# Layer 0's gate and up products by a scheme of seven products for eight, with Silu in both halves

## The chip, the cores and the metric

The kernel runs on one core of one Trainium2 chip. The metric is the device time of one execution in microseconds (us): the median of several runs, beside one execution taken with the hardware profiler. The engines are TensorE (PE; its weight loads are listed as PEld), VectorE (DVE), ScalarE (ACT), GpSimd (POOL) and SyncE (SP, which issues most DMAs). Each runs its own instructions in order; they wait for each other by semaphores.

## What is computed

Two layers on x of shape (4, 256, 256), all in float32. Layer 0 is an attention of 16 heads and a gated feed-forward; layer 1 is an mLSTM with a gated feed-forward of its own, and then a feed-forward with int8 weights. The change is in layer 0's feed-forward (`fwht` is a normalized Walsh-Hadamard transform; W1 and W3 are 1024 x 256):

```python
up_gate = jnp.einsum('bsd,hd->bsh', x, W1)
up_lin = jnp.einsum('bsd,hd->bsh', x, W3)
hidden = jax.nn.silu(up_gate) * up_lin
hidden = fwht(hidden)
out = jnp.einsum('bsh,dh->bsd', hidden, W2)
...
x = _layernorm(x + _L0_attn_ref(x, ...), axis=-1)
x = _layernorm(x + _L0_ffn_ref(x, ...), axis=-1)
x = _layernorm(x + _L1_attn_ref(x, ...), axis=-1)
x = _layernorm(x + _L1_ffn_ref(x, ...), axis=-1)
```

## The kernel before

The 1024 tokens are two halves of 512 tokens, that is of two batches of 256. P is 128, KC = 2 chunks of the 256 features, NH = 8 chunks of the 1024 hidden features.

**Attention, 0 to about 407 us.** It goes by 16 blocks, one for each pair of heads and half. The projections of the next block (`fast_projections`) already use a scheme of seven products for eight: a 2x2 block product, over two output chunks and two batches, is built from seven block products with sums of inputs (`input_sums`, kept in `xsum`) and of weights (`weight_sums`, kept in `wsums`, on VectorE at the end of every even block). Each partial result accumulates in one of two PSUM banks, "x" and "y"; ScalarE copies what is in x to where it is wanted, VectorE adds what is in y. The steps A1 to A7 and B1 to B7 are issued in an order written out by hand (`ORDER`, and `EARLY` for blocks 0 and 1), between the scores, the products with the values (V) and the output products (O). Block 1 uses `EARLY[1]`. The banks of the B steps (tag "sc") are those that block 1's first scores lie in. GpSimd does the rotary products (L298 to L300) and, before the last block, the Hadamard butterflies of W2 between chunks; four matrix products (`hadamard`) do those within a chunk, the last two at about 408 us.

**Layer 0's feed-forward** (`ffn0`, with `glu` and `down`) is written as a generator for each half: layernorm, transposes, then for every hidden chunk two products of 512 columns for the gate and two for the up part, a Tanh on ScalarE, (tanh + 1) times the gate and times the up part on VectorE (silu(v) is v/2 times (tanh(v/2) + 1); the half is taken in `down`), then four rows of eight down products of 256 columns. Half 0's up part (410 to 437 us) runs by itself.

**Half 1 and the mLSTM.** Half 1's stream is filler for the first half of the mLSTM. `merge` takes the number that `mlstm` yields, which is how many microseconds of other TensorE work should stand there, and pulls pieces from the other stream until their own yields (1.7 for half a chunk of `glu` or half a row of `down`) have paid it; the program order comes out of these counts. The engines' queues follow it, except where something later was ready first. `mlstm(0)` asks for 9.0, 1.7, 0, 1.7, 1.7, 3.4, 1.7, 3.4, 9.0 and 1.7, and 4.3 more are asked for after it, around the norm with which `ffn1(0)` begins. What then is left of the stream follows the transposes of `ffn1(0)`. After that, `ffn1(0)` is filler for `mlstm(1)` in the same way.

**ScalarE in the mLSTM.** `gates` needs Exp, Ln and Exp after a Tanh; `decays` needs 8 Exps of 128x128 in each of four groups. A group is queued behind the newest gate activation traced so far (`evictions[-1]`, L1003). GpSimd prepares the Exps' input (L995), from maxima that come back by DMA.

**Buffers.** Weights and sums of 8 KB a partition share the tag "ff" with seven buffers, each taken when one is free, in program order. ScalarE's functions are read from a table; when the one that is wanted isn't in the table that is loaded, an ACT_TABLE_LOAD stands before it.

Of the kernel before, what the change touches and what calls it, by code (L numbers as in the profile page):

```python
# [25 lines left out]
NH = FF // P  # L26
HALF = NT // 2
NJH = HALF // P
# [11 lines left out]
def tile_two_layers(ctx: ExitStack, tc: tile.TileContext, a: dict, out: bass.AP):  # L40
    nc = tc.nc
# [5 lines left out]
    def bank(tag):  # L47
        return psum.tile([P, 512], F32, tag=tag, name=f"ps_{tag}")
# [90 lines left out]
    def ff_weight(name, engine=nc.sync, dtype=F32):  # L139

        tiled = [P, NH, D] if name in ("w2", "w_down", "q_down") else [P, KC, FF]
        t = wts.tile(tiled, dtype, tag="ff", name=name, bufs=7)
        src = a[name]
        engine.dma_start(t, src.bitcast(mybir.dt.int8) if src.dtype == I32 else src)
        return t

    xsum = wts.tile([P, 2, 4, S], F32, tag="ff", name="xsum", bufs=7)
    wsums = [wts.tile([P, 4, 4 * P], F32, tag="ff", name=f"wsum{k}", bufs=7) for k in range(2)]
# [10 lines left out]
    settled = {}  # L159
    behind = lambda ins: tc.issue_after(ins.ins)  # L160
    nothing = lambda: None

    def projections(h):

# [367 lines left out]
    def output_product(h, bb, po):  # L532
# [24 lines left out]
    ORDER = "A1 A2 V00 A6 V01 A7 A5 B1 B2 A3 A4 B6 B7 V10 B5 V11 O0 B3 O0 B4 O1 O1".split()  # L557
    EARLY = {
        0: "A1 A2 B1 A6 B2 A7 A5 B6 A3 B7 B5 A4 B3 B4".split(),
        1: "A1 A2 B1 B2 A6 A7 B6 B7 A5 B5 V00 A3 V01 A4 B3 B4 V10 V11 O0 O0 O1 O1".split(),  # L560
    }
    def fast_block(h, t, probs, prev, steps):

# [66 lines left out]
    for h in range(NB - 1):  # L630
        if h and h % 2 == 0 and h // 2 + 1 < NPAIR:
            with behind(settled["block"]):
                weight_sums(h // 2 + 1)
        probs = fast_block(h, tiles, probs, prev, steps)
        if h % 2 == 0:
            if 0 < h < NB - 2:
                w_os[h // 2 + 1] = load_output(h // 2 + 1)
            if h // 2 + 2 < NPAIR:
                weights[h // 2 + 2] = load_pair(h // 2 + 2)
        prev, tiles = tiles, after_it  # L640
        if h + 2 < NB:
            after_it, steps = fast_projections(h + 2)

# [153 lines left out]
            nc.vector.tensor_tensor(hT[:, c, :], pu, g, ALU.mult)  # L797
            yield 1.7

    def down(hT, wd, j, tag, rows):  # L800

        po = bank(tag)[:, :D]
        for i in range(NH):
            nc.tensor.matmul(  # L804
                po, lhsT=hT[:, i, j * P : (j + 1) * P], rhs=wd[:, i, :], start=(i == 0), stop=(i == NH - 1)
            )
            if i == NH // 2 - 1:
                yield 1.7
        with tc.issue_after(chained[-1].ins) if chained else contextlib.nullcontext():
            nc.vector.scalar_tensor_tensor(rows, po, 0.5, rows, ALU.mult, ALU.add)  # L810
        yield 1.7

    def ffn0(n, tag):
        fm, hT = feature_major(n), hidden(n, hid)
        layernorm(acc[n], acc[n])
        yield 0.0
        transposed(acc[n], fm, tag)
        yield 0.9
        yield from glu(fm, w1, w3, hT, tag)
        for j in range(NJH):  # L820
            yield from down(hT, w2h, j, tag, acc[n][:, j, :])
        layernorm(acc[n], xb[n])

    def ffn1(n, tag):

        h2 = work.tile([P, NJH, D], F32, tag="hin", name=f"h2_{n}")
        rmsnorm(acc[n], h2)
        yield 0.0
        fm, hT = feature_major(n), hidden(n, hid)
        evicted = transposed(h2, fm, tag, vecs[:, 4:6])  # L830
        with tc.issue_after(evicted.ins):
            for j in range(NJH):
                nc.vector.tensor_tensor(xs[n][:, j, :], acc[n][:, j, :], xb[n][:, j, :], ALU.add)
        yield 0.9
        yield from glu(fm, w_gate, w_up, hT, tag)
        for j in range(NJH):
            yield from down(hT, w_down, j, tag, xs[n][:, j, :])
            if j % 2:
                layernorm(xs[n][:, j - 1 : j + 1], xb[n][:, j - 1 : j + 1], 2)

# [15 lines left out]

    def mlstm_in(n, t):

        hin = work.tile([P, NJH, D], F32, tag="hin", name=f"hin{n}")
        rmsnorm(xb[n], hin)  # L860
        yield 10.5 if n else 9.0
        fm = feature_major(n)
# [209 lines left out]
    def run(stream):  # L1072
        for _ in stream:
            pass

    def take(count, stream):
        return itertools.islice(stream, count)
# [160 lines left out]
            yield from s  # L1238

    hid = tc.alloc_tile_pool(name="hid", bufs=2)  # L1240
    up = 2 + 2 * NH
# [137 lines left out]
```

## Time and profile before

| what | value |
|---|---|
| median of 3 runs | 697.17 us (694.35 to 697.26) |
| the profiled execution | 697.11 us, span 695.3 us |
| mean granted TensorE clock | 0.992 |
| ScalarE busy, 409.8 to 437.2 us (half 0's gate and up) | 5.5 us |
| ScalarE busy, 451.9 to 526.2 us (half 1 with the mLSTM) | 28.2 us |
| VectorE busy, 451.9 to 526.2 us | 51.2 us |
| table loads of ScalarE | 7 in all: one at the start, four in the mLSTM, two in the last feed-forward |
| HBM read | 25.61 MB, 38 GB/s over the span |

The profile's page gives the busy time of each engine as a share of the span, the chain of work that ended last, and groups of instructions by line, engine and operation. A line of a timeline has start (us), duration (us), engine, source line, operation, output and inputs with their shapes, and how many records were merged; an idle time before it stands in brackets with what ended it. A wait line has who waited for whom: us in total, times, the longest. The products of the helper that all of them share are at L70, so they are told apart by their tiles: `ps_d` is a PSUM bank of the feed-forwards, `ps_m` of the mLSTM.

### The profile page before, as it was taken

The numbers are of one execution on the slowest core, as the hardware profiler recorded it, in microseconds if no ns is written. First come the engines' busy times: TensorE is split into PE (matmuls) and PEld (weight loads), VectorE is DVE, ScalarE is ACT, GpSimd is POOL, SyncE is SP. The second block draws the span as 40 slices with busy tenths as digits, with TensorE's granted clock in tenths as the row PEclk, the third lists the DMA queues.
The fourth block names the chain that finished last, engine by engine and source line by source line (L and its number), as shares of the span: only waits on it lengthen the run. The fifth ranks groups of instructions, "written<-read, shape, count | busy, mean of one in ns | idle before, by whom it ended". The sixth has DMA issues, their size and how long they took to land.

```text
span 695.3 us, 9871 instructions
## 1 busy us (share of the span) xinstructions
PE 685.8 (99%) x3408; PEld 533.6 (77%) x3408; DVE 451.3 (65%) x1242; ACT 260.3 (37%) x773; POOL 177.4 (26%) x187
## 2 busy tenths in 40 slices
PE   9999999999999999999999999999999999999995
PEld 5888988988888898888889764845685458648885
DVE  5966666577478568567547664273779459835767
ACT  2442543354254244325425331037212561111652
POOL 4244404422730740742143000005000130000210
PEclk9999999999999999999999999999999999999998
DMA  8543233332321521531432451003030300000001
GB/s 271 213 122 60 42 96 61 59 94 46 84 85 30 136 47 22 131 61 24 113 62 39 144 106 27 0 1 122 1 122 0 123 1 1 0 0 1 1 0 61
DMA packets 49026, 45.43 MB, mean 65 GB/s; under 512 B 9520, under 2 KB 42704, under 8 KB 47824
## 3 DMA queue, kind: packets, MB, share of 16 engines
q1 hardware_dynamic: 48112, 41.00, 22.8%
q0 software_dynamic: 432, 3.15, 1.3%
q10 hardware_dynamic: 432, 0.66, 0.3%
q8 instruction: 27, 0.44, 0.3%
q14 instruction: 23, 0.19, 0.1%
HBM read 25.61 MB, written 1.08 MB: 38 GB/s over the span
## 4 chain that ended last, share of the span: by engine, by line
PE 97%; DVE 2%; ACT 1%; issue 0%; DVEq 0%; ACTq 0%
PE ps_mm L354 13%; PE ps_d L70 12%; PE ps_mm L70 9%; PE ps_m L70 8%; PE ps_ot L70 8%; PE ps_sc L346 6%; PE ps_sc L354 6%; PE ps_d L804 6%; PE ps_sc L438 4%; PE ps_pt L438 4%; PE ps_d L1117 4%; PE ps_sc L450 2%; PE ps_m L1036 2%; PE ps_m L804 2%; PE ps_pt L450 2%; PE ps_m L773 1%
## 5 line engine op out<-in xcount | busy, mean ns | idle before, releaser
L298 POOL TENSOR_TENSOR rope_raw<-rope_raw,cst 128x512 f32<-128x512 f32 x30 | 38.2, 1274 | 187.8 <-DVE rope_swp L295 187.8
L470 ACT ACTIVATE pr<-ps_sc,nmax 128x256 f32<-128x256 f32 x64 | 29.7, 474 | 121.3 <-DVE nmax L461 121.3
L70 PE MATMUL ps_mm<-w_o,oT 128*128 128x256 f32 x256 | 62.2, 379 | 0.0
L70 PE MATMUL ps_ot<-prT,v 128*128 128x256 f32 x240 | 61.4, 380 | 0.2 <-issue 0.2
L70 PE MATMUL ps_d<-fm,w 128*128 128x512 f32 x128 | 58.1, 606 | 0.0
L552 DVE TENSOR_TENSOR acc<-ps_mm,acc 128x512 f32<-128x512 f32 x32 | 22.1, 691 | 49.8 <-PE ps_mm L70 49.6
L70 PEld LDWEIGHTS ps_mm<-w_o,oT 128*128 128x128 f32 x256 | 46.7, 190 | 5.3
L995 POOL TENSOR_TENSOR ex<-cst,ex 128x512 f32<-128x512 f32 x16 | 19.7, 1263 | 110.8 <-DMA ex<-far 66.1
L70 PEld LDWEIGHTS ps_ot<-prT,v 128*128 128x128 f32 x240 | 43.3, 190 | 5.5 <-issue 0.9
L70 PEld LDWEIGHTS ps_d<-fm,w 128*128 128x128 f32 x128 | 24.2, 192 | 27.5 <-issue 25.6
L461 DVE TENSOR_REDUCE nmax<-ps_sc 128x2 f32<-128x512 f32 x32 | 20.6, 685 | 36.2 <-PE ps_sc L450 36.0
L354 PE MATMUL ps_mm<-xsum,wsum 128*128 128x256 f32 x180 | 43.9, 380 | 0.0
L488 DVE STREAM_TRANSPOSE cross<-pr 128x512 f32<-128x512 f32 x60 | 42.6, 710 | 1.4
L368 ACT COPY kn<-ps_sc 128x256 f32<-128x256 f32 x56 | 20.9, 373 | 58.3 <-PE ps_sc L346 58.2
L480 DVE TENSOR_SCALAR pr<-pr,rinv 128x256 f32<-128x256 f32 x128 | 39.1, 347 | 1.6
L795 ACT ACTIVATE glu_g<-ps_d 128x512 f32<-128x512 f32 x24 | 14.2, 594 | 67.8 <-PE ps_d L70 67.8
L299 POOL TENSOR_TENSOR rope_swp<-rope_swp,cst 128x512 f32<-128x512 f32 x30 | 38.2, 1275 | 0.0
L354 PEld LDWEIGHTS ps_mm<-xsum,wsum 128*128 128x128 f32 x180 | 33.9, 190 | 4.5
L377 DVE TENSOR_TENSOR kn<-ps_sc,kn 128x256 f32<-128x256 f32 x42 | 17.8, 424 | 28.6 <-ACT kn L368 18.1
L1113 POOL TENSOR_TENSOR qh<-gq,qh 128x512 fp32r<-128x512 f32 x6 | 7.8, 1294 | 96.4 <-issue 84.7
L470 ACT ACTIVATE pr<-ps_pt,nmax 128x256 f32<-128x256 f32 x64 | 30.1, 488 | 2.5 <-DVE nmax L461 2.5
L438 PE MATMUL ps_sc<-kn,qn 128*128 128x256 f32 x128 | 30.2, 379 | 0.0
(271 smaller groups left out, 1567.0 us busy)
## 6 DMA issues: line engine op xcount, KB each, us to landing
prT<-cross SPq DMA_DIRECT2D x240, 64.0 KB, 2.1
w_qkv<-in_w_qkv SPq DMA_DIRECT2D x7, 1024.0 KB, 5.4
ex<-far SPq DMA_DIRECT2D x8, 512.0 KB, 5.6
w<-in_w SPq DMA_DIRECT2D x3, 1024.0 KB, 12.4
w_o<-in_w_o SPq DMA_DIRECT2D x8, 256.0 KB, 3.0
acc<-in_x SPq DMA_DIRECT2D x2, 512.0 KB
w_gate<-in_w_gate SPq DMA_DIRECT2D x1, 1024.0 KB
w_up<-in_w_up SPq DMA_DIRECT2D x1, 1024.0 KB, 5.1
```

Source lines behind the costliest of these rows:

```text
L70: last = nc.tensor.matmul(ps, lhsT=lhs(i), rhs=rhs(i), start=(i == 0), stop=(i == n - 1))
L298: nc.gpsimd.tensor_tensor(by_b(raw[c]), by_b(raw[c]), cs, ALU.mult)
L299: nc.gpsimd.tensor_tensor(by_b(swp), by_b(swp), sn, ALU.mult)
L346: lambda: nc.tensor.matmul(ps[:, k * S + j * P : k * S + (j + 1) * P], lhsT=x[:, j * P : (j + 1) * P], rhs=wt, start=(start and not k and ...
L354: lambda: nc.tensor.matmul(ps[:, k * S : (k + 1) * S], lhsT=wt, rhs=x, start=(start and not k), stop=True, skip_group_check=True,)
L438: lambda: nc.tensor.matmul(ps[bb][e][:, qt * S : (qt + 1) * S], lhsT=qn[:, e, queries(bb, qt)], rhs=kn[:, e, keys(bb)], start=(qt == 0), s ...
L450: lambda: nc.tensor.matmul(ps[bb][e][:, qt * S : (qt + 1) * S], lhsT=qr[rows, queries(bb, qt)], rhs=kr[rows, keys(bb)], start=False, stop= ...
L470: nc.scalar.activation(pr[:, qt, :], ps[:, qt * S : (qt + 1) * S], AF.Exp, bias=nmax[:, qt : qt + 1], accum_out=rsum[:, qt : qt + 1],)
L480: nc.vector.tensor_scalar(pr[:, qt, :], pr[:, qt, :], rinv[:, qt : qt + 1], None, ALU.mult)
L488: return nc.vector.transpose(cross[:, :, e], pr.rearrange("p t (x i) -> p x t i", i=32))
L804: nc.tensor.matmul(po, lhsT=hT[:, i, j * P : (j + 1) * P], rhs=wd[:, i, :], start=(i == 0), stop=(i == NH - 1))
L1117: nc.tensor.matmul(ps, lhsT=lhs, rhs=rhs, start=(k == 0), stop=(k == len(terms) - 1))
```

## The change

Layer 0's gate and up products take the scheme of seven products that the attention has. A "pair" is two hidden chunks; for each of the four pairs, each of the seven products is made for the gate and for the up weights, over 256 columns. Gate and up share a bank. `fast_glu` steps through the pairs in an order written out by hand (`STEPS`: first digit the pair, second the product); "--" pulls the first half of the first down row forward.

```diff
+    def hidden_sums(engine, ws, which):
+        for x, w in enumerate(ws):
+            part = lambda i, c: w[:, i, :].rearrange("p (k c d) -> p k c d", c=2, d=P)[:, :, c, :]
+            one, two = gsum[:, 0, x], gsum[:, 1, x]
+            if which == "first":
+                engine.tensor_tensor(one, part(0, 1), part(1, 1), ALU.add)
+                engine.tensor_tensor(two, one, part(0, 0), ALU.subtract)
+            elif which == "third":
+                engine.tensor_tensor(gsum3[:, x], part(0, 0), part(0, 1), ALU.subtract)
+            else:
+                engine.tensor_tensor(part(0, 1), part(1, 0), two, ALU.subtract)
...
-        1: "A1 A2 B1 B2 A6 A7 B6 B7 A5 B5 V00 A3 V01 A4 B3 B4 V10 V11 O0 O0 O1 O1".split(),
+        1: "A1 A2 A6 A7 B1 B2 A5 B6 B7 B5 V00 A3 V01 A4 B3 B4 V10 V11 O0 O0 O1 O1".split(),
...
+        if h == NB - 3:
+            gsum = wts.tile([P, 2, 2, NH // 2, P], F32, tag="ff", name="gsum", bufs=7)
+            with behind(settled["block"]):
+                hidden_sums(nc.vector, (w1, w3), "first")
...
+    gsum3, tsum = more_sums()
+    for which in ("third", "fourth"):
+        hidden_sums(nc.gpsimd, (w1, w3), which)
...
-    w_gate, w_up = ff_weight("w_gate"), ff_weight("w_up")
-    w_down = ff_weight("w_down")
+    w_up, w_gate = ff_weight("w_up"), ff_weight("w_gate")
...
+    def token_sums(xT):
+        tok = lambda i, b: xT[:, i, b * S : (b + 1) * S]
+        one, two, three, four = (tsum[:, m, :] for m in range(4))
+        nc.vector.tensor_tensor(one, tok(0, 1), tok(0, 0), ALU.subtract)
+        nc.vector.tensor_tensor(two, tok(1, 1), one, ALU.subtract)
+        nc.vector.tensor_tensor(three, tok(1, 1), tok(0, 1), ALU.subtract)
+        return nc.vector.tensor_tensor(four, tok(1, 0), two, ALU.subtract)
+
+    STEPS = (
+        "01 02 11 06 12 07 05 16 17 03 04 15 21 22 13 26 14 27 25 31 32 23 36 37 24 35 -- 33 34"
+    ).split()
+
+    def fast_glu(xT, wg, wu, hT, tag, silu, other):
+        def pair(k):
+            g, banks, batch = [], {}, lambda b: slice(b * S, (b + 1) * S)
+            def products(name, m):
+                start = m in (1, 2, 7)
+                if m < 3:
+                    banks[name] = bank(tag)
...
+                    nc.tensor.matmul(
+                        banks[name][:, batch(x)], lhsT=left, rhs=right,
+                        start=start and not x, stop=True, skip_group_check=True,
+                    )
...
+            def copy(c, b):
+                for x, to in enumerate(places(c, b)):
+                    nc.scalar.copy(to, banks["x"][:, batch(x)])
+            def add(c, b):
+                for x, to in enumerate(places(c, b)):
+                    nc.vector.tensor_tensor(to, banks["y"][:, batch(x)], to, ALU.add)
+            def gated(c, b, found=None):
+                gate, to = places(c, b)
+                at_g, at_u = found or (gate, to)
+                if silu:
+                    evictions.append(nc.scalar.activation(gate, at_g, AF.Silu))
+                else:
+                    th = gate if found else work.tile([P, S], F32, tag="junk", name="glu_th")
+                    evictions.append(nc.scalar.activation(th, at_g, AF.Tanh, scale=0.5))
+                    nc.vector.scalar_tensor_tensor(gate, th, 1.0, at_g, ALU.add, ALU.mult)
+                nc.vector.tensor_tensor(to, at_u, gate, ALU.mult)
+            def step(m):
+                products("x" if m in (1, 6, 5, 3) else "y", m)
+                if m == 1:
+                    copy(0, 0)
+                elif m == 2:
+                    add(0, 0)
+                    gated(0, 0)
+                elif m == 6:
+                    copy(1, 0)
+                elif m == 5:
+                    copy(1, 1)
+                    add(1, 1)
+                    gated(1, 1)
+                elif m == 3:
+                    gated(0, 1, (banks["x"][:, batch(0)], banks["x"][:, batch(1)]))
+                elif m == 4:
+                    add(1, 0)
+                    gated(1, 0)
+            return step
+        pairs = [pair(k) for k in range(NH // 2)]
+        for s in STEPS:
+            if s == "--":
+                yield next(other)
+            else:
+                pairs[int(s[0])](int(s[1]))
+                yield 0.86
...
-        yield from glu(fm, w1, w3, hT, tag)
+        token_sums(fm)
+        silu = True
+        rows = [down(hT, w2h, j, tag, acc[n][:, j, :], 1.0 if silu else 0.5) for j in range(NJH)]
+        yield from fast_glu(fm, w1, w3, hT, tag, silu, rows[0])
...
-        h2 = work.tile([P, NJH, D], F32, tag="hin", name=f"h2_{n}")
+        h2 = work.tile([P, NJH, D], F32, tag="hin", name=f"h2_{n}", bufs=1)
...
-    run(take(up - 2, one))
+    run(take(len(STEPS), one))
...
-    q_gate, q_up, q_down = (ff_weight(k, nc.gpsimd, F32R) for k in ("q_gate", "q_up", "q_down"))
+    w_down = ff_weight("w_down")
+    q_gate, q_up = (ff_weight(k, nc.gpsimd, F32R) for k in ("q_gate", "q_up"))
...
+    q_down = ff_weight("q_down", nc.gpsimd, F32R)
     run(take(1 + 2 * NH + 2 * NJH - 3, one))
```

The fourth weight sum overwrites the weight block that it replaces. `gsum`, and one buffer for `gsum3` and the token sums `tsum`, take two of the seven "ff" buffers. So layer 1's weights come into other buffers, and some later. The layer 1 feed-forward keeps `glu` with its Tanh.

More of the change, by code (lines that the diff above doesn't have):

```diff
@@ L145, in ff_weight @@
         return t
+    pair_sums = lambda k: wts.tile([P, 4, 4 * P], F32, tag="ff", name=f"wsum{k}", bufs=7)
+    wsums = [pair_sums(0)]
     xsum = wts.tile([P, 2, 4, S], F32, tag="ff", name="xsum", bufs=7)
-    wsums = [wts.tile([P, 4, 4 * P], F32, tag="ff", name=f"wsum{k}", bufs=7) for k in range(2)]
+    wsums.append(pair_sums(1))
     w2b = wts.tile([P, NH, D], F32, tag="ff", name="w2b", bufs=7)
@@ L161, in tile_two_layers, with more_sums @@
     nothing = lambda: None
+    def more_sums():
+        both = wts.tile([P, 8 * S], F32, tag="ff", name="gsum3", bufs=7)
+        return (
+            both[:, 0 : 4 * S].rearrange("p (x k d) -> p x k d", x=2, k=NH // 2),
+            both[:, 4 * S :].rearrange("p (m s) -> p m s", m=4),
+        )
[10 more added lines that the diff above has]
+                engine.tensor_tensor(part(0, 1), part(1, 0), two, ALU.subtract)
     def projections(h):
@@ L798, in glu @@
             yield 1.7
-    def down(hT, wd, j, tag, rows):
+    def token_sums(xT):
[5 more added lines that the diff above has]
+        return nc.vector.tensor_tensor(four, tok(1, 0), two, ALU.subtract)
@@ new lines, in tile_two_layers, with places @@
+    STEPS = (
[8 more added lines that the diff above has]
+                    banks[name] = bank(tag)
+                tok = lambda i, b: xT[:, i, batch(b)]
+                for x, w in enumerate((wg, wu)):
+                    block = lambda c, i: w[:, i, (2 * k + c) * P : (2 * k + c + 1) * P]
+                    left, right = {
+                        1: lambda: (block(0, 0), tok(0, 0)),
+                        2: lambda: (block(0, 1), tok(1, 0)),
+                        3: lambda: (block(1, 0), tok(1, 1)),
+                        4: lambda: (block(1, 1), tsum[:, 3, :]),
+                        5: lambda: (gsum[:, 0, x, k], tsum[:, 0, :]),
+                        6: lambda: (gsum[:, 1, x, k], tsum[:, 1, :]),
+                        7: lambda: (gsum3[:, x, k], tsum[:, 2, :]),
+                    }[m]()
+                    nc.tensor.matmul(
+                        banks[name][:, batch(x)], lhsT=left, rhs=right,
+                        start=start and not x, stop=True, skip_group_check=True,
+                    )
+            def places(c, b):
+                if not g:
+                    g.append(work.tile([P, 2, HALF], F32, tag="glu_g", name="glu_g"))
+                return g[0][:, c, batch(b)], hT[:, 2 * k + c, batch(b)]
+            def copy(c, b):
[40 more added lines that the diff above has]
+                yield 0.86
@@ L802, in down @@
+    def down(hT, wd, j, tag, rows, scale=0.5):
         po = bank(tag)[:, :D]
@@ L809, in down @@
         with tc.issue_after(chained[-1].ins) if chained else contextlib.nullcontext():
-            nc.vector.scalar_tensor_tensor(rows, po, 0.5, rows, ALU.mult, ALU.add)
+            nc.vector.scalar_tensor_tensor(rows, po, scale, rows, ALU.mult, ALU.add)
         yield 1.7
@@ L818, in ffn0 @@
         yield 0.9
-        yield from glu(fm, w1, w3, hT, tag)
+        token_sums(fm)
+        silu = True
+        rows = [down(hT, w2h, j, tag, acc[n][:, j, :], 1.0 if silu else 0.5) for j in range(NJH)]
+        yield from fast_glu(fm, w1, w3, hT, tag, silu, rows[0])
         for j in range(NJH):
-            yield from down(hT, w2h, j, tag, acc[n][:, j, :])
+            yield from rows[j]
         layernorm(acc[n], xb[n])
     def ffn1(n, tag):
-        h2 = work.tile([P, NJH, D], F32, tag="hin", name=f"h2_{n}")
+        h2 = work.tile([P, NJH, D], F32, tag="hin", name=f"h2_{n}", bufs=1)
         rmsnorm(acc[n], h2)
@@ L834, in ffn1 @@
         yield 0.9
+        rows = [down(hT, w_down, j, tag, xs[n][:, j, :]) for j in range(NJH)]
         yield from glu(fm, w_gate, w_up, hT, tag)
         for j in range(NJH):
-            yield from down(hT, w_down, j, tag, xs[n][:, j, :])
+            yield from rows[j]
             if j % 2:
@@ L857, in mlstm_in @@
     def mlstm_in(n, t):
-        hin = work.tile([P, NJH, D], F32, tag="hin", name=f"hin{n}")
+        hin = work.tile([P, NJH, D], F32, tag="hin", name=f"hin{n}", bufs=1)
         rmsnorm(xb[n], hin)
@@ L1240, in tile_two_layers @@
     hid = tc.alloc_tile_pool(name="hid", bufs=2)
-    up = 2 + 2 * NH
     one, other = ffn0(0, "d"), ffn0(1, "d")
```

## The prediction

> **What bounds the kernel now.** I read the page's busy shares first, then the waits of TensorE, then the chain of work that ended last, then the timelines of the stages that the change touches.
>
> ```profile
> PE 685.8 (99%) x3408; PEld 533.6 (77%) x3408; DVE 451.3 (65%) x1242; ACT 260.3 (37%) x773; POOL 177.4 (26%) x187
> ...
> PE 97%; DVE 2%; ACT 1%; issue 0%; DVEq 0%; ACTq 0%
> ```
>
> ```profile
> PE ps_sc L354 <- ACT pr L470: 1.0, 1, 1.0
> ```
>
> TensorE is busy for 685.8 of 695.3 us and is 97% of the chain; the second fence (all waits of TensorE above a microsecond) holds one entry. So a product removed shortens the kernel, unless TensorE then waits for something that the product was covering. The chain gives the prices:
>
> ```profile
> 409.93 27.47 PE ps_d L70 x64
> 438.27 13.82 PE ps_d L804 x64
> 452.08 11.16 PE ps_d L70 x26
> ```
>
> A product leaves two records, so the first line is the 32 products of half 0's gate and up, 27.47/32 = 0.858 us each over 512 columns; the second is 32 products over 256 columns, 13.82/32 = 0.432 us each, with another weight load each. The third opens half 1, whose products are woven into the first mLSTM half until 526 us.
>
> **The products.** Per half, 32 x 0.858 = 27.5 us go; 4 pairs x 7 x 2 (gate, up) = 56 products of 256 columns come, 56 x 0.432 = 24.2. Gain 3.3 us a half, 6.6 in all. Their weight loads, 0.19 us a record, hide behind 0.432 us as L804's do. That a step of seven runs at this pace is shown by the attention, which already does it: one block lasts 24.67 us, time after time in the chain, with no wait.
>
> **The sums.** The first weight sums are 4 operations of 128x512 on VectorE in block 13; L268 to L271 start 0.47 us apart for 384 columns, so 512 cost about 0.62, together 2.5 us. Where the attention makes its own sums (310 to 313 us) no TensorE wait follows, and block 13 has none of those: VectorE idles 3.8 us before the next maxima (338.86). Taken at nothing; uncovered, 2.5 us. The other sums are 4 GpSimd operations of 128x512, at L298's 1.27 us 5.1 us, when the attention's sums are read for the last time (about 383 us); GpSimd is idle from 383 to 407 and their first reader comes after 410. Nothing; at worst 2 us if VectorE's softmax nearby is slowed (its 128x384 sums took 0.68 beside GpSimd, 0.55 without). The token sums are 4 x about 0.4 us on VectorE, ready two steps before use: nothing, uncovered 1.6.
>
> **Block 1's order.** The one 1.0 us wait lies at 45.19: B1 wants the bank that the first exponentials (44.1 to 45.1) read. A6 and A7, 4 products or 1.7 us, now come before it, and what they wait for, A1's copies and A2's adds, had ended at 42.1 and 43.1. Gain 1.0, between 0 and 1.0.
>
> **Buffers and queues.** The gate weights' load, issued on SP at 336, now waits for a buffer until the Hadamard products end (410); first read 526. The down weights' load waits until about 522; read 580, landing 6.9 us. Behind it on SP stand the second half's gmax copies, about 543. GpSimd issues its three loads (0.5 to 0.7 us each) at other times, the last after the second mLSTM half, first read 665. The single input buffer is rewritten only after its transposes. All nothing; the price of a late megabyte would be its 5 to 12 us.
>
> **Half 0.** A pair has 6 PSUM copies and 4 Silus on ScalarE, 10 x 0.28 us (the pitch of L368's and L370's copies) = 2.8, and 10 VectorE operations at a pitch of 0.34 = 3.4, beside 6.0 us of products. They fit. The Silu table is loaded once, in ScalarE's idle time. At the end the last pair's add, Silu and multiply (about 1.9 us) stand behind 8 transposes (0.87) and three down products (1.3): I take 0.3 us of waiting, between 0 and 1.
>
> **Half 1, ScalarE.** The mLSTM around it needs Exp, and the new steps need Silu, where the old gate had Tanh. What a switch costs:
>
> ```profile
> 467.15 0.41 ACT L931 ACTIVATE lsp<-gt 64x256 f32<-64x256 f32 x1
> 467.58 1.28 ACT L932 ACT_TABLE_LOAD   x1
> 468.88 0.42 ACT L932 ACTIVATE lsp<-lsp 64x256 f32<-64x256 f32 x1
> ...
> 480.08 5.94 ACT L1007 ACTIVATE ex<-ex,tok 128x128 f32<-128x128 f32 x20
> 485.93 0.58 ACT L795 ACTIVATE glu_g<-ps_d 128x512 f32<-128x512 f32 x1
> 486.40 2.44 ACT L1007 ACTIVATE ex<-ex,tok 128x128 f32<-128x128 f32 x8
> ```
>
> ScalarE is full here from 480 to 489, without a switch, as Tanh came between Exps unloaded. Each of the four `decays` groups (8 Exps, 2.4 us) is ordered behind the newest Silu (L1003). Counting the yields that `merge` weighs, steps 22 and 13 fall between the first two groups, 26 and 14 between the next, 27, 25, 31 and 32 before the last: silu, exp three times over, and silu again after it, 7 loads.
>
> ```profile
> 478.40:491.95 13.55, 13.55 (x89) 8.95 (x88) 6.71 (x13) 11.19 (x37) 8.54 (x7) 1.00 0.13 50
> 491.95:500.10 8.15, 8.15 (x46) 3.87 (x46) 5.99 (x20) 1.72 (x4) 0.00 (x0) 0.79 0.00 1
> ```
>
> In these windows (length, then busy PE, PEld, DVE, ACT, POOL, clock) ScalarE works 11.2 + 1.7 = 12.9 of 21.7 us, to the start of the second `attend`. Out go 3 Tanhs at 0.5; in come up to there 8 copies and 5 Silus at about 0.3 (3.9) and 6 loads (7.7): 12.9 - 1.5 + 3.9 + 7.7 = 23.0, over the 21.7. ScalarE becomes the bound here, by 1.3 us. One more load stands before the first Exp of the gate chain, which runs through two scans and two DMAs to GpSimd's start at 477.08: 1.3 us later, with little slack behind it. Together 2.6 us. From below, nothing: the copies may slip in where ScalarE idles. From above 7 us, if steps queue behind Exp groups: step 25 needs 26's copy, 35 needs 36's. I take 2.6; the sum of work is the nearer bound because TensorE has other steps to take meanwhile.
>
> [...] The row shows no drain: the load starts 0.02 us after the Exp before it ends, and Ln starts 0.02 after the load. [...]
>
> **Half 1, the cover.** These products also hid the mLSTM's own latencies. The end, by TensorE's timeline:
>
> ```profile
> 518.80 4.91 PE L804 MATMUL ps_d<-w,hT 128*128 128x256 f32 x22
> 523.54 1.04 PE L773 MATMUL ps_d<-cst,h 128*128 128x128 f32 x8
> 524.42 1.89 PE L804 MATMUL ps_d<-w,hT 128*128 128x256 f32 x8
> 526.15 1.88 PE L70 MATMUL ps_d<-fm,w_gate 128*128 128x512 f32 x4
> ```
>
> Three half rows (5.2 us) cover the norm between w_out and the transposes, one (1.7) the eviction after them. The norm's last rows come at 523.1, just before the transposes. The stream is now 24.1 + 13.6 = 37.7 us by its own counts against 40.8, and merge asks for 37.6: it runs dry two half rows earlier, one missing before the transposes and one after. The first costs its 1.7 us, the second about 1.1 (eviction to 525.5 against the transposes' end at 524.4). I take 2.8, between 0 and 3.4.
>
> **The sum** on the profiled execution, 697.1 us (span 695.3 and 1.8 around it; the median shown is 697.17, and 694.35 the lowest): 697.1 - 6.6 - 1.0 + 0.3 + 2.6 + 2.8 = 695.2. Half 0 pays; half 1 gives its gain back.
>
> **The rivals.**
> *ScalarE is hidden* (0.24). It had only 60% of its stage; if the switches find its idle time, only the cover and the tail are lost: 697.1 - 7.6 + 0.3 + 1.5 = 691.3. For it: TensorE never waits in the stage now, and there are steps to take out of turn. Against: the Exps are already packed, and the order behind L1003 forces the switches.
> *ScalarE starves TensorE* (0.26), the slower one: between 478 and 500 us the copies that release a PSUM bank queue behind a load, eight Exps and another load, 1.3 + 2.4 + 1.3 = 5.0 us, where the interleaving leaves a copy 1.7 us. Three such meetings at 5.0 - 1.7 = 3.3 us are 9.9 in place of 2.6: 702.5. It decides once more than one meeting in three finds no other step ready. For it: the banks of two pairs are all there are. The clock adds to it: after the first `attend` it was granted at 0.79 over 8.15 us, 1.7 us lost, and idle stretches may bring more of that.
> *That the order above holds* (0.50): 695.2, from 692.5 to 698.
>
> **Numbers.** About 0.5%, 3.5 us, is what a measurement of this kernel can tell from no change. The likeliest case puts 0.40 within it and 0.10 faster; the hidden case is faster (0.24); the starved one is slower (0.20) or within (0.06). Faster 0.34, same 0.46, slower 0.20. Range 690.5 to 701.
>
> **What would show it.** Half 0's products last about 24.2 us without a wait, and block 1's wait is gone. About seven table loads lie between 478 and 505 us, with waits of PE for ScalarE's copies or VectorE's adds. TensorE idles 2 to 3 us around the transposes before the second glu. I am wrong if the loads come bunched (few), if a load takes 2.7 us, or if half 0 waits.

## The result and the profile after

The changed kernel is slower. Its profiled execution takes 706.58 us (span 704.8) beside 697.11 (span 695.3) for the kernel before. The median of the first four runs is 709.98 us (702.55 to 714.74) against 697.21, and the ratio is 1.0117, interval [1.0072, 1.0162]; in a later batch it was 705.29 (702.82 to 706.65) beside 697.19, ratio 1.0126 [1.0077, 1.0175]. The runs of 713.37 and 714.74 us, at a granted clock of 0.973, are left out of the first ratio, which so rests on those of 702.55 and 706.58 (clock 0.991 and 0.982).

The busy shares and the chain of the kernel after:

```profile
PE 688.3 (98%) x3504; PEld 556.1 (79%) x3504; DVE 466.5 (66%) x1302; ACT 290.0 (41%) x847; POOL 182.3 (26%) x191
...
PE 81%; DVE 9%; ACT 4%; DMA 3%; POOL 1%; issue 1%; SPq 0%; DVEq 0%; ACTq 0%; POOLq 0%
```

TensorE was to be busy for some 6 us less and is busy for 2.5 us more: a busy time grows when products run at a lower clock (below, four records take 2.07 us at 0.50 where four took 1.13 at full clock). Its part of the chain fell from 97% to 81%: the chain now runs through other engines. All its waits above half a microsecond, after:

```profile
PE ps_d L867 <- ACT hT L879: 3.8, 1, 3.8
PE ps_d L804 <- DVE h L795: 1.8, 1, 1.8
PE ps_pt L82 <- PEq L1499: 0.8, 1, 0.8
PE ps_d L70 <- DVE fm L811: 0.7, 1, 0.7
PE ps_m L804 <- DVE hin L795: 0.6, 1, 0.6
```

The wait for the exponentials in block 1 has gone from the list. In its place, where before it had nothing in half 1, stands a wait of 3.8 us for a copy by ScalarE (L879), then the waits around the norm at the end of the mLSTM half (1.8 and 0.7) and one for its input norm (0.6). The 0.8 us at the very start was there before.

Half 0 in the chain of the kernel after (start, length, line, records):

```profile
410.07 22.45 PE ps_d L867 x104
432.51 1.73 PE ps_d L930 x8
434.24 1.73 PE ps_d L867 x8
```

The 112 records take 22.45 + 1.73 = 24.2 us, the 24.2 of the prediction, and no wait breaks them.

The longest wait, on ScalarE's timeline and then on TensorE's, after (start, length, line, operands):

```profile
482.36 1.28 ACT L1137 ACT_TABLE_LOAD   x1
483.66 2.45 ACT L1137 ACTIVATE ex<-ex,tok 128x128 f32<-128x128 f32 x8
486.01 0.35 ACT L879 COPY glu_g<-ps_d 128x256 f32<-128x256 f32 x1
```

```profile
481.71 1.13 PE L867 MATMUL ps_d<-gsum 128*128 128x256 f32 x4
486.68 2.07 PE L867 MATMUL ps_d<-gsum,gsum 128*128 128x256 f32 x4 [3.84 <-ACT hT L879]
```

Step 26's copies (486.01) stand in ScalarE's line behind a table load and a group of eight Exps. Step 25 writes on into the same bank and waits for them, and TensorE does nothing in the meantime. Its first four records afterwards take 2.07 us where four took 1.13 before the wait. The same stretch by windows (length, then busy PE, PEld, DVE, ACT, POOL with instructions, clock, DMA share, GB/s):

```profile
482.60:486.68 4.08, 0.24 (x2) 0.00 (x0) 3.67 (x8) 4.05 (x12) 3.97 (x4) 0.80 0.00 0
486.68:491.90 5.22, 5.22 (x12) 4.16 (x13) 0.63 (x2) 5.18 (x11) 0.00 (x0) 0.50 0.00 0
491.90:495.30 3.40, 3.40 (x32) 3.36 (x31) 0.00 (x0) 1.54 (x6) 0.00 (x0) 1.00 0.00 0
495.30:502.00 6.70, 6.70 (x31) 5.22 (x31) 3.68 (x10) 4.29 (x8) 0.00 (x0) 0.50 0.01 2
```

The clock falls inside the wait, stays at 0.50 for 5.2 us of work behind it, is full during the first `attend` (third row: products of 33 columns, weights loading all the time), and is at 0.50 again for 6.7 us behind that. A third stretch (532.9 to 539.7) follows the waits at the end of the half. Before, half 1 had one such stretch of 3.4 us, behind its first `attend`.

**Where the time went.** In steps of 0.25 us I split each stage into idle time of TensorE, loss to the clock (busy time x (1 - granted clock)) and the rest, work at full clock:

| us | before | after | difference |
|---|---|---|---|
| start to half 0's first product | 409.77 | 409.90 | +0.1 |
| half 0's layer 0 | 42.15 | 38.87 | -3.3 |
| half 1's layer 0 with the mLSTM, work | 72.52 | 71.77 | -0.75 |
| the same, TensorE idle | 0.0 | 7.1 | +7.1 |
| the same, lost to the clock | 1.7 | 6.1 | +4.4 |
| from there to the end | 169.15 | 171.0 | +1.9, of it clock 1.3 |
| span | 695.3 | 704.8 | +9.5 |

The gain is there (-3.3 - 0.75). It is outweighed by 7.1 us of waits and by 5.7 us of half clock (4.4 + 1.3). This split is that of one execution. The fastest runs of the changed kernel, 702.55 and 702.82 us, have the granted clock (0.991 and 0.992) at which the kernel before takes some 697.3, and are still 5 us slower. So the clock is not the whole of the loss; in runs with less half clock, part of it may come back as longer waits, which no trace here shows.

### The profile page after: what moved, and what is told of

The parts are those of the page before. It is cut to its first block, busy times and chain, and to the rows that moved or that the text cites. A ratio compares the mean times of both kernels' runs of the same rounds, so it can differ in the third digit from the quotient of the medians.

```text
span 704.8 us, 10217 instructions
## 1 busy us (share of the span) xinstructions
PE 688.3 (98%) x3504; PEld 556.1 (79%) x3504; DVE 466.5 (66%) x1302; ACT 290.0 (41%) x847; POOL 182.3 (26%) x191
## 4 chain that ended last, share of the span: by engine, by line
PE 81%; DVE 9%; ACT 4%; DMA 3%; POOL 1%; issue 1%; SPq 0%; DVEq 0%; ACTq 0%; POOLq 0%
PE ps_mm L378 12%; PE ps_ot L70 8%; PE ps_mm L70 8%; PE ps_sc L370 6%; PE ps_sc L378 6%; PE ps_d L867 5%; PE ps_m L70 5%; PE ps_d L930 4%; PE ps_d L70 4%; PE ps_d L1247 4%; PE ps_sc L462 3%; PE ps_pt L462 3%; PE ps_sc L474 2%; PE ps_m L1166 2%; PE ps_m L930 2%; PE ps_pt L474 2%
## 5 line engine op out<-in xcount | busy, mean ns | idle before, releaser
L504 DVE TENSOR_SCALAR pr<-pr,rinv 128x256 f32<-128x256 f32 x128 | 42.8, 376 | 1.7
L462 PE MATMUL ps_pt<-kn,qn 128*128 128x256 f32 x128 | 30.2, 379 | 0.0
L930 PE MATMUL ps_d<-w,hT 128*128 128x256 f32 x128 | 29.5, 381 | 0.0
L370 PEld LDWEIGHTS ps_sc<-wsum,xsum 128*128 128x128 f32 x168 | 25.4, 191 | 2.2
```

The costliest lines, as they stand in the source:

```text
L370: lambda: nc.tensor.matmul(ps[:, k * S + j * P : k * S + (j + 1) * P], lhsT=x[:, j * P : (j + 1) * P], rhs=wt, start=(start and not k and ...
L462: lambda: nc.tensor.matmul(ps[bb][e][:, qt * S : (qt + 1) * S], lhsT=qn[:, e, queries(bb, qt)], rhs=kn[:, e, keys(bb)], start=(qt == 0), s ...
L504: nc.vector.tensor_scalar(pr[:, qt, :], pr[:, qt, :], rinv[:, qt : qt + 1], None, ALU.mult)
L930: nc.tensor.matmul(po, lhsT=hT[:, i, j * P : (j + 1) * P], rhs=wd[:, i, :], start=(i == 0), stop=(i == NH - 1))
```

## The experiments

**The theories.** Theory W: half 1 lost its time to waits alone, because ScalarE, with seven table loads, could not keep up. Theory C: the waits are half of it; a TensorE that stands still (3.8 us in the kernel after) or has little to stream (an `attend` lasts 3.66 us in the kernel before) lowers the granted clock behind that, for 3.4 us in the kernel before and 6.8 in the kernel after, so a wait costs more than its length. Rival to both: only the lost cover matters. (In the expectations W is the stall theory and C the clock theory; the first four, written before the two were told apart, have "theory S" for the table switches and "rival C" for the cover.) The kernel before ran beside every batch. Its own runs lie in groups near 694.3 (clock 0.997), 697.2 (0.991 to 0.994) and 699.8 us (0.989), so that its median of 697 holds 2 to 3 us more of lost clock than its best runs.

**Half 1 with Tanh** (Silu in half 0 alone, the products as changed).

```diff
-        silu = True
+        silu = not n
```

> The change with Tanh instead of Silu in half 1 alone (two table loads beside before's seven, where the change has ten). Theory S (the switches between Silu and Exp hold back ScalarE's copies, TensorE runs dry and its clock falls): the 3.8 us wait for the copy of step 25 goes, and with it one or two stretches at half clock; the end of half 1 still waits about 2.5 us. Time 693 to 697. Rival C (the missing cover does it, or the seven-product steps in general, by their many evictions): the waits and the half clock stay, 702 to 706.

Measured: 696.0 us (694.5 to 699.28), ratio 1.0012 [0.9991, 1.0034]. With 9 table loads in place of 17, the wait for step 26's copy is 1.7 us, the stage's idle time 3.5 instead of 7.1, and there is no half-clock stretch in it at all. The waits at the end of the half are shorter too:

```profile
PE ps_d L70 <- DVE fm L811: 0.7, 1, 0.7
PE ps_d L804 <- DVE h L795: 0.4, 1, 0.4
```

So the Silu in half 1 costs the changed kernel about 9 us by the medians (8 by the ratios), as both theories have it; they part in what those consist of.

**Half 0 alone** (half 1 keeps the products of before, on weights of which one block holds a sum, so its values differ).

```diff
...
-        yield from fast_glu(fm, w1, w3, hT, tag, silu, rows[0])
+        if n:
+            yield from glu(fm, w1, w3, hT, tag)
+        else:
+            yield from fast_glu(fm, w1, w3, hT, tag, silu, rows[0])
```

> The seven-product scheme in half 0 alone; half 1 goes by glu with Tanh as before, on weights of which one block in four holds a sum (its values differ, its work is before's). Both theories: the gain of half 0 comes through whole, 3.3 us, 693.9, and half 1 shows before's profile: no wait, one or two short stretches at half clock. If it is near 697 the added sums and buffers cost something elsewhere.

Measured: 697.83 (697.03 to 701.13), ratio 1.0022 [1.0008, 1.0036]. A miss of both theories. Half 0's 3.3 us are there in the trace (it takes 38.86 us instead of 42.15) and TensorE waits for only 0.8 us in half 1, but the granted clock of the runs is 0.984 to 0.993. The profiled run, the slowest of the 16, has 8.5 us of half-clock loss in stretches that each begin towards the end of an `attend`, against 3.4 in the profiled run before. This pointed to the attends.

**The kernel before with Silu in half 1**, nothing else.

```diff
-            evictions.append(nc.scalar.activation(g, pg, AF.Tanh, scale=0.5))
-            nc.vector.scalar_tensor_tensor(g, g, 1.0, pg, ALU.add, ALU.mult)
+            if silu:
+                evictions.append(nc.scalar.activation(g, pg, AF.Silu))
+            else:
...
```

> The kernel before, with Silu in place of Tanh in half 1 alone: six more table loads, no product gone, no copies. Theory S in its plain form (loads cost ScalarE time in the stage): a wait of TensorE in the mLSTM of 1 to 4 us and a stretch at half clock, 699 to 703. Rival (loads alone are hidden, it takes the copies of the scheme too, since 512-wide products leave ScalarE four times the slack): 697, no wait.

Measured: 698.29 (696.19 to 702.02), ratio 1.0041 [1.0024, 1.0058]; 13 loads. The Silu alone costs the old products 1.5 us by the medians (2.9 by the ratio), with waits of 1.6 us in the stage and no more half clock than before, where it costs the new ones 8 to 9: there are fewer Silus between the Exps (21 Exps stay together), and no copies that a bank waits for. So most of the loss needs both parts of the change.

**The kernel before with less cover** (four products of 512 columns of half 1 left out, 3.4 us).

```diff
+            few = cut and c >= NH // 2
-            mm_k(pg, lambda i: wg[:, i, cols], lambda i: xT[:, i, :], KC)
+            mm_k(pg, lambda i: wg[:, i, cols], lambda i: xT[:, i, :], 1 if few else KC)
```

> The kernel before with four of half 1's products left out (the second feature chunk of the gate in hidden chunks 4 to 7), 3.4 us of TensorE work, and nothing else changed. Rival C (cover): about 2.8 us come back as waits at the end of half 1, and if a wait drops the clock, 1.7 to 3.3 more: 696 to 700. If cover is worth nothing: 693.8.

Measured: 694.21 (693.49 to 695.05), ratio 0.9978 [0.9968, 0.9989]. Waits at the end of the half of 0.4 + 0.7 us appear, not 2.8. By this the cover is worth about 1 us, as in the form with Tanh (0.4 + 0.7 there), and the rival falls.

**The wait filled with useless products** (after, step 27 of half 1 done five times).

```diff
-                pairs[int(s[0])](int(s[1]))
+                for _ in range(1 + fill if s == "27" else 1):
+                    pairs[int(s[0])](int(s[1]))
...
```

> The changed kernel, with step 27 of half 1 (two products of 256 columns, its bank overwritten with the same values) done five times in place of once, ahead of step 25: some 3.5 us of needless products stand where TensorE waited 3.8 us for step 26's copy. Clock theory (an idle or sparse stretch of a few us halves the granted clock for the 3.4 or 6.8 us after it): the half-clock stretch at 485 to 492 goes, the added work costs nothing, and the time falls by about 3.4 us, to some 703 beside the 706.6 of the profiled run before it. Stall theory (the wait alone cost its 3.8 us, the clock is chance): the time stays at 706 to 707, and the half-clock stretches stay. If the wait did not bound anything: 710.

Measured: 699.45 (698.29 to 703.76), ratio to before 1.0036 [1.0023, 1.0049]; the granted clock is 0.991 to 0.996. Some 3.5 us of added work make the kernel 6 us faster than the 705.3 that the unfilled one took beside the same kernel before in the next batch. TensorE's timeline where the wait was:

```profile
481.59 4.58 PE L867 MATMUL ps_d<-gsum 128*128 128x256 f32 x20
486.94 1.13 PE L867 MATMUL ps_d<-gsum,gsum 128*128 128x256 f32 x4 [0.77 <-ACT hT L879]
```

The 3.8 us wait shrinks to 0.8, a new one of 1.3 comes later, and there is no half clock from 478 to 502 us. In the profiled run, the slowest of the 23, the stage's work at full clock and its idle time together are 1.0 us more than unfilled (+3.1 and -2.1); only the loss to the clock is less, 1.7 us in place of 6.1. Theory W forbids this; theory C asked for some 703 and was too cautious.

**The attends parted, in the kernel before.**

```diff
             for half in range(2):
                 attend(t, bb, half, hv)
-            if not bb:
-                decays(t, 1, 1)
-                yield 1.7
+                if not half:
+                    if not bb:
+                        decays(t, 1, 1)
+                    yield 1.7
...
-        yield 9.0
+        yield 7.3
```

> The kernel before, with 1.7 us of feed-forward products between the two calls of attend of each batch (taken from the yield after them and from the 9.0), so that 32 products of 33 columns no longer follow one another; the third decays group is issued after the first call. Clock theory: the two half-clock stretches that follow attend (492 and 567, 1.71 us each) go, the time is 693 to 694.5, and the runs at 697 and 700 go too. Rival (the stretches come by chance and not from attend): 696 to 697.5, stretches still there.

What the edit is aimed at, in the kernel before (windows as above):

```profile
488.50:492.25 3.75, 3.75 (x34) 3.73 (x33) 2.52 (x5) 1.18 (x5) 0.00 (x0) 1.00 0.02 4
492.25:495.60 3.35, 3.35 (x12) 1.10 (x14) 1.73 (x5) 1.03 (x3) 0.00 (x0) 0.53 0.00 0
```

By the first row PE is never idle, but it is loading weights as long as it multiplies (PEld 3.73 of 3.75): 33 columns per load. The next 3.35 us are granted half the clock. Measured with the attends parted: 696.98 (696.26 to 697.5), ratio 1.0001 [0.9985, 1.0017]. The clock rose, as theory C says: 0.997 or 0.998 in 10 of 14 runs, where 20 of 59 runs of before reach 0.997, and the runs at 699 and above are gone. The profiled run (0.994) still has one such stretch, at 495.53. The time did not follow and is what the rival had forecast: the lowest is 2.2 us above the lowest of before, and in the profiled run half 1's work at full clock is 73.66 us in place of 72.52. What the new order pays there, I did not settle.

**The attends parted, half 0 alone.** The edit of the last, on the form with half 0 alone.

> The kernel with the seven products in half 0 alone (half 1 by the products of before, on weights of which one block has been overwritten, so its values differ), with attend's two calls parted as in the kernel before parted. The unparted one took 697.83 where half 0's gain of 3.3 us asked for 693.9, with 8.5 us of half-clock loss in stretches that each begin at the end of an attend. Clock theory: those go, 692 to 694.5. Rival (the loss lies elsewhere, or the clock falls anyway): 696.5 to 698.

Measured: 695.99 (694.73 to 699.61), ratio 0.9992 [0.9972, 1.0012]; clock 0.991 to 0.998, up from 0.984 to 0.993. The time lies between the two forecasts: the 1.8 us won are less than hoped for. The order has its price here too (half 1's work at full clock is 73.8 us for 73.1 unparted), and the profiled run, the slowest, still has 10.2 us at half clock from 490.23, behind a wait of 0.8 us and the first call of `attend`.

**The attends parted, Tanh in half 1.**

> The changed kernel with Tanh in half 1 (Silu in half 0), with attend's two calls parted. Unparted: 696.0, two waits of 1.7 and 0.7 us. Clock theory: the runs that lost 1.7 to 5 us to half-clock stretches after attend lose them no more; 692.5 to 694.5, the fastest of all valid forms so far. Rival (ScalarE is the bound in half 1 even with Tanh, and parting only moves its waits): 695.5 to 698.

Measured: 700.31 (697.37 to 702.26), 4.3 us more than unparted. The rival was nearer: the waits grow (5.5 us idle in the stage for 3.45, 1.8 of it before the transposes of the second norm).

**The loads taken away** (after, the first half's decays by Tanh, which needs no load beside Silu; their values differ).

```diff
-                        ex[:, h, c, :], ex[:, h, c, :], AF.Exp, bias=...
+                        ex[:, h, c, :], ex[:, h, c, :], t["func"], bias=...
...
-        t = {}
+        t = {"func": AF.Exp if n else AF.Tanh}
```

> The changed kernel with the decays of the first half's mLSTM computed by Tanh in place of Exp (their values differ): ScalarE has the same instructions, but six of the seven table loads between the decays and the Silus, 7.7 us of it, are not needed. If the loads are what makes ScalarE the bound in half 1: the waits of TensorE there shrink to those of the form with Tanh in the products (3 us), the half-clock stretches go with them, and the time is 694 to 698. Rival (the copies and the order of the steps starve TensorE, whatever the loads): 702 or more.

Measured: 698.62 (696.18 to 702.67), ratio 1.0024 [1.0004, 1.0044]: 6.7 us below the changed kernel in the same batch, with the same instructions on ScalarE but the loads. The waits go from 7.1 to 4.3 us, the clock loss in the stage from 6.1 to 3.4. A wait of 2.5 us for the copy stays, so the loads are not all of it.

**The changed kernel again.**

> The changed kernel as it is, beside the others of this batch. Clock theory: its 3.8 us wait and its attends meet the window of the clock differently in each run, so that its times lie in steps of 1.7 us between 702 and 715, the granted clock of a run falling with its time; median about 706 to 710.

Measured: 705.29 (702.82, 704.05, 706.52, 706.65; clock 0.992, 0.986, 0.982, 0.982). Its profile repeats the three half-clock stretches within 0.2 us of their places, and a wait of 4.1 us at step 25.

**Block 1's order alone, in the kernel before.**

```diff
-        1: "A1 A2 B1 B2 A6 A7 B6 B7 A5 B5 V00 A3 V01 A4 B3 B4 V10 V11 O0 O0 O1 O1".split(),
+        1: "A1 A2 A6 A7 B1 B2 A5 B6 B7 B5 V00 A3 V01 A4 B3 B4 V10 V11 O0 O0 O1 O1".split(),
```

> The kernel before with the changed kernel's order of block 1 alone. By the trace of the changed kernel (0.24 and 0.28 us of new waits at B6 and B7 in place of the one of 0.96): 0 to 0.4 us less than before. By the prediction's step: 1.0 us less.

Measured: 696.62 (694.06 to 699.71), ratio 0.9992 [0.9966, 1.0018]. The 1.0 us wait is exchanged for two of 0.3 and 0.2 us at B6 and B7. The lowest runs (694.06 and 694.08) agree to 0.1 us. No gain of 1.0 is to be seen; one of 0.4 would be lost in the interval.

**TensorE held, first attempt** (the kernel before; one product of ffn1 waits for six useless copies by ScalarE).

```diff
+            if hold and c == 2:
+                slow = work.tile([P, HALF], F32, tag="glu_g", name="slow")
+                for _ in range(hold):
+                    held = nc.scalar.copy(slow, pg)
...
-            mm_k(pu, lambda i: wu[:, i, cols], lambda i: xT[:, i, :], KC)
+            mm_k(pu, lambda i: wu[:, i, cols], lambda i: xT[:, i, :] if i else first, KC)
```

> The kernel before, in which one group of products of ffn1's first half (its third up product) waits for six copies of a bank by ScalarE, which nothing else needs, and one copy of its operand: TensorE, dense before and after, stands still for some 4 us once. Clock theory: 4 us and a half-clock stretch of 3.4 or 6.8 us behind it (1.7 or 3.4 us lost): before plus 5.5 to 7.5. Stall theory: before plus 4, no stretch at half clock behind it.

Measured: 698.32 (697.53 to 699.27), ratio 1.0024 [1.001, 1.0037]. It tests nothing: other products and transposes were put ahead of the held one, and TensorE idled for 0.7 us.

**TensorE held for 1.8 and for 4.3 us, at a dense place** (half 0's layer 0; the edit of the last there, with every later product of that half behind the held one; two and six copies).

```diff
-            mm_k(pg, lambda i: wg[:, i, cols], lambda i: xT[:, i, :], KC)
+            with late():
+                mm_k(pg, lambda i: wg[:, i, cols], lambda i: xT[:, i, :], KC)
...
+            if hold and c == 2:
+                late = lambda: tc.issue_after(done.ins)
```

> The kernel before, in which one up product of half 0's layer 0 waits for two copies of a bank by ScalarE that nothing needs and a copy of its operand; every later product of that half is kept behind it, so that TensorE, dense on both sides, stands still for about 2 us once. [...] Stall theory: the same 2 us. If a wait of any length lowers the clock: before plus 3.5 or more.

> The same with six copies: TensorE stands still for about 4.4 us once, some 10 us into half 0's products, where the kernel before and the changed kernel both run at full clock. Clock theory: a half-clock stretch of 3.4 or 6.8 us begins in or behind the wait in nearly every run, so before plus 5.5 to 7.5. Stall theory: before plus 4.4, the clock full around it.

The short hold by windows, then the long one:

```profile
418.65:420.46 1.81, 0.00 (x1) 0.00 (x1) 0.00 (x0) 1.74 (x4) 0.00 (x0) 1.00 0.64 192
420.46:425.00 4.54, 4.54 (x11) 2.15 (x12) 1.49 (x3) 1.04 (x2) 0.00 (x0) 1.00 0.07 9
```

```profile
419.00:423.37 4.37, 0.09 (x1) 0.00 (x0) 0.00 (x0) 4.08 (x8) 0.00 (x0) 0.83 0.33 89
423.37:428.20 4.83, 4.83 (x6) 2.18 (x7) 1.38 (x2) 0.45 (x1) 0.00 (x0) 0.50 0.00 0
428.20:434.00 5.80, 5.80 (x14) 2.48 (x13) 1.58 (x3) 1.19 (x2) 0.00 (x0) 0.96 0.00 0
```

After 1.81 us of standing still the clock is 1.00; after 4.3 it is 0.50 for 4.8 us of products, of which 2.4 are lost (4.83 x 0.5). Measured: 698.24 (696.15 to 705.35), ratio 1.0031 [1.0011, 1.0051], and 704.16 (702.28 to 704.9), ratio 1.0092 [1.0063, 1.012]. The long hold costs 6.9 us for 4.3 of waiting, the short one 1.0 by the medians and 2.0 by the lowest runs for 1.8. For a standstill of 4.3 us theory C is shown, at a place where neither ScalarE's loads nor an attend is near.

**The second decays group one step later** (after).

```diff
         for k, _ in enumerate(zip(*carried)):
             yield 1.7
-            if not k:
+            if k:
                 decays(t, 0, 1)
```

> The changed kernel with the second group of decays of half 0's mLSTM issued one step of that stream later, behind the copy of step 26: ScalarE then does 16 Exps in one go, with five table loads in place of seven. The 3.8 us wait for step 26's copy goes. If ScalarE as a whole is the bound in that stretch, the wait comes back for a later copy (that of step 25, which then stands behind 16 Exps), 2 to 4 us long, less the 2.6 us of two loads: 700 to 706. If only the order in the line was wrong: 696 to 699.

ScalarE's timeline then:

```profile
482.30 0.36 ACT L890 ACTIVATE glu_g<-ps_d 128x256 f32<-128x256 f32 x1
482.56 0.36 ACT L879 COPY glu_g<-ps_d 128x256 f32<-128x256 f32 x1
...
484.45 1.28 ACT L1137 ACT_TABLE_LOAD   x1
485.75 4.79 ACT L1137 ACTIVATE ex<-ex,tok 128x128 f32<-128x128 f32 x16
```

Step 26's copy now comes straight after the Silu, and two groups of Exps share one load. Measured: 699.31 (697.41 to 703.74), ratio 1.0043 [1.0027, 1.006], 6 to 7 us below the changed kernel. The waits for copies are 0.9 us in all, those of the stage 3.1. I had expected the wait to come back at step 25's copy, behind 16 Exps: it does so for half a microsecond only, as an `attend` of 3.9 us lies in between. So the order of ScalarE's line made the long wait, more than its whole load. The new order also saves two loads, but six loads less in the old order left a wait of 2.5 us. The clock is 0.984 to 0.993 all the same: stretches at 491 and 502 us, behind the two attends.

**The same with Tanh in half 1.**

> The form with Tanh in half 1 (696.0), with the same later issue of the decays. If ScalarE's order alone made its wait of 1.7 us: 694 to 695. If the wait only moves to the next copy: 695.5 to 697.

Measured: 696.35 (695.25 to 697.49), ratio 0.9986 [0.9963, 1.0009]. The 1.7 us wait for the copy is gone; 1.0 us for the decays' product on VectorE takes its place, as the second forecast has it. No run is at full clock (0.989 to 0.993).

**Both late forms with the attends parted.**

> The changed kernel with the later second group of decays (699.3) and with attend's two calls parted. Clock theory: its two half-clock stretches, each at an attend (1.7 us each), go, and the parted order costs the 2 us that it cost the kernel before: 696.5 to 699.5, with the granted clock at 0.995 or more and a smaller spread.

> The form with Tanh in half 1 and the later decays (696.35, granted clock 0.989 to 0.993 in all runs), with attend's two calls parted: 693.5 to 696 if the half-clock stretches of 3.4 us go and parting costs 2 us or less; 696 to 698 if parting moves ScalarE's and VectorE's waits as it did in the form without the later decays (700.3).

Measured: 704.19 (698.76, 700.73, 707.66 and 710.29), ratio 1.0135 [1.0071, 1.0199], and 701.01 (697.66 to 703.7), ratio 1.0053 [1.0028, 1.0077]. Two misses. In the first one's timeline 30 of the first 32 products of the attend still follow one another, so it does not test what it was made for, and what drives its spread stays open. In the second they are parted, but the waits before the second norm's transposes are back (1.8 us).

## Why the prediction was wrong

It said 695.2 us, at most 701; the profiled execution took 706.6. None of its three signs of being wrong came, and still it was. Term by term:

- **Half 0's products, -3.3 and a tail of 0.3**: right, -3.3, and no tail.
- **The sums, nothing**: right. GpSimd did its four between 333.9 and 341.1 us, not at 383, and TensorE did not wait for them or for VectorE's.
- **Half 1's products, -3.3**: too much. The stage's work at full clock falls by 0.75 us, and by 1.2 in the form with Tanh, whose stage has no half clock. There the 112 records take 0.232 us each, for 0.216 in half 0, which is 1.8 us more, in gaps too short for the list of waits. The rate was read from a stage without another stream and carried into one with it. The products that went were slower in half 1 too, though (0.443 us a record for 0.429 in half 0): 28.3 us went and 25.9 came, or 25.3 in the changed kernel with the half clock taken out, a gain of 2.4 to 3.1. The rest was lost by products that the sum left alone: in the changed kernel half 1's down products take 0.7 us more than before and the mLSTM's scores (L1150) 1.3, as half of these now start two at a time and not four (from 495.65 to 502.9). Why the gaps and this order come was not tried.
- **Block 1's wait, -1.0**: a new wait took its place (0.5 us in two pieces), and block 1 ends at 68.34 us, where it ended at 68.18 before. The exchange of order alone gained nothing measurable.
- **Half 1's waits, +2.6 and +2.8**: 7.1 us. ScalarE's 2.6 became 3.8 in one place, because "TensorE has other steps to take meanwhile" failed: its line is in order, and step 25 stood at the head of it. The starving rival had named that very meeting, "step 25 needs 26's copy". Seven loads came as counted. For the cover 2.8 came out at 2.5, by luck: with Tanh the same missing cover cost 1.1, so 1.4 of the 2.5 came with the Silu. That a load takes 1.28 us with no gap behind it holds too: 482.36 + 1.28 ends 0.02 us before the Exp at 483.66. All 24 loads in the profiles before and after (7 and 17) take 1.28 us; no run shows one of the 2.7 us that the prediction has among its signs.
- **The clock, 0 in the sum**: 5.7 us. The prediction had the row (0.79 over 8.15 us behind the first `attend`) and wrote "idle stretches may bring more of that", but gave it no price, not even in the rival, which so ended at 702.5 instead of some 706. A price could be taken from that row, 1.7 us for one such stretch; the stretches in the kernel after are twice as long (6.83 us at 0.50, 485.07 to 491.90 and twice more).

Two steps failed, then. **The largest single miss is the clock, put at nothing without a reason and measured at 5.7 us** of the 11.4 between forecast and measurement. **The other is half 1 itself**: the steps that TensorE was to take meanwhile were not there, so that it waited for 7.1 us in place of 5.4, and the gain in work was 0.75 us in place of 3.3. By the runs at the clock of the kernel before, 702.6 and 702.8 us, the second alone seems enough to leave the range.

Within one execution the half-clock stretches begin whole steps of 3.41 us apart: at 485.07, 495.31 and 532.86 in the kernel after (3 and 11 steps), at 492.45 and 567.54 in the kernel before (22 steps). Each lasts two steps (6.83 us) in the kernel after and one (3.41 us) in the kernel before. The steps lie differently in each execution: the first of these begin 0.38 and 0.93 us past a multiple of 3.413, that of the long hold 2.04. So the steps don't start with the kernel, which fits the groups of run times of one and the same program.

What fills the step before a fall differs. The one before the first fall still had 1.2 us of products in the kernel after (481.66 to 485.07) and 0.6 in the long hold; in the kernel before it had no idle time, and its products were of 33 columns up to 491.95 (489.04 to 492.45). In the filled run, steps counted back from the fall at 502.08 put a border at 491.84, which cuts the same `attend` (489.63 to 493.2) in two, and no half clock follows. The length of a wait alone does not decide it: 1.8 us amid dense products left the clock full (1.00 in the short hold), and 1.8 us in the step before 532.86, with 1.64 us of products and transposes beside them, did not. A look at idle gaps alone would not have found the attends: there the engine counts as busy throughout (3.75 of 3.75 us), and the clock falls behind them. What sets the clock is not shown beyond this.

That the clock rises and falls with the form is shown by the filled wait (work added, 6 us won) and by the held products. For the attends it is shown less strictly: parting them raised the clock in the kernel before and in the form with half 0 alone, but the new order costs about as much as the clock gives.

None of the forms with the seven products beats the kernel before beyond its interval; nearest are the Tanh form with later decays (0.9986) and half 0 alone with parted attends (0.9992, with half 1 on altered weights).

## What to carry to other kernels

Where TensorE is dense, price a wait of about 4 us at its length plus what the half clock behind it loses (here 2.6 us behind the wait of 3.8 and about as much behind that of 4.3; nothing behind 1.8 amid dense products), and look for it where a PSUM copy stands in one engine's line behind work of another stream; moving one group of instructions by one step, which also saved two table loads, won back 6 us here, most of what the change had lost. A fast product scheme pays in a stage of its own (half 0: the full 3.3 us), and much less where it is woven into a latency-bound stream. Before crediting a saving of 3 us, look at how far apart the runs of one program lie: here those of the kernel before move by 3 to 5 with the granted clock.

## What the hardware showed that I had not expected

- Products of 33 columns, one weight load each, for 3.66 us: PE busy 100%, then 3.41 us at clock 0.50 (before: 492.45 to 495.86).
- Needless products can shorten a kernel: some 3.5 us added, 6 us gained.
- Amid dense products a standstill of 1.8 us left the clock at 1.00; one of 4.3 us cost 6.9 us.
- The half-clock stretches of one execution begin whole steps of 3.41 us apart, and the steps lie differently in each execution.
- Tanh beside Silu needs no table load: with the decays by Tanh, six of the seven loads in the stretch went away.
